# A pair of blocks 1 and 0, earlier joins, and turning inside products, in a two-layer graph kernel

## The chip, the cores and the metric

The kernel runs on one core of a Trainium2 chip. The metric is the time of one execution on the device, in microseconds (us). The engines are named as in the profile: PE is TensorE (matrix products), DVE is VectorE, ACT is ScalarE, POOL is GpSimd, and SP is SyncE, which here only issues transfers. Every engine works through its own list of instructions in a fixed order, which is settled when the kernel is built.

## The reference

The input is x (2708 x 1024, float32) and adj (2708 x 2708, only zeros and ones, with few ones and very uneven rows). Two layers follow one another, and the output is that of the second.

```python
# layer 0
q = x @ W_q.T + b_q;  k = x @ W_k.T + b_k;  v = x @ W_v.T + b_v
z = (1 / sqrt(1024)) * (q @ k.T) * adj
z = where(z == 0, -10000, z)
x = layernorm(x + relu(softmax(z, axis=1) @ v))
# layer 1
x = layernorm(x + adj @ (x @ weight) + bias)
```

A row takes part only in the products with its neighbours, the ones of its row in adj. A row without neighbours gets the mean of all v.

## The kernel before

The rows are sorted by their number of neighbours into 22 blocks of 128 rows (the last has 20), and the list SLOTS (L32) says how many neighbours a block's rows have at most. Blocks 0 to 7 are one family, blocks 8 to 21 another, each from heavy to light; block 21 has no neighbours. The 32 heaviest rows of block 0, the "hub", have their neighbours dealt over four times as many lanes, and their shares are joined later.

The kernel never forms q, k and v of all rows. For layer 0 it takes M, the product of the transposed W_q with W_k (L609), while VectorE lists the ones of adj. Then y = x M, with a bias row, block by block of x in its given order (y_block, L288: products L319, eviction by VectorE L323, write to memory; loads of x at L280). The score of a row with a neighbour is the dot product of the row of y and the row of x (VectorE, L813). The softmax weights sum the neighbours' rows of x into a row r (VectorE, L870), and only r is multiplied by W_v. Rows without neighbours take the mean of x, whose columns are summed by ScalarE from the blocks of x in y_block (column_sums, L330 and L332) and scaled by VectorE (L294, L295). Layer 1 likewise sums the neighbours' rows of x1, layer 0's output in memory (sum_rows, L1226, VectorE at L1238 and L1241), and then multiplies by the weight.

Neighbours' rows are fetched by GpSimd, which issues one indirect transfer per slot of a block (L343, L349): 128 rows, 512 KB. It also scatters finished rows (L703).

To be multiplied, r must be turned: TensorE transposes four pieces of 128 x 128 into one of three banks (pool p_tr, L716), ScalarE copies the bank out (L717), and so twice for a block. Block 0 is turned and joined with its hub at once, by products with matrices of ones and zeros that carry the shares' weights (flip_shares, L729 to L731). Accumulating products have four banks (pool p_o).

There are three kinds of product in layer 0. A single block ("v") takes 16 matmuls (project, L739) and is finished by finish0 (L900). The last block's product with the mean is project_mean (L752), in four quarters that are put together at L761. A pair ("p") of blocks takes seven products of halves instead of eight, each of 4 matmuls (half_products, L999), in the manner of Strassen: it needs four sums of quarters of the two turned blocks (S, L988 to L991, VectorE), three differences of quarters of W_v and one quarter overwritten by a difference (L1136 to L1139, VectorE, once), and seven additions (L1011, VectorE). finish_pair (L1063) adds x and takes the sums for the norm (L1069). A norm ends on ScalarE with a square (L775), small steps in turn on ScalarE and VectorE, and a scaling (L788); then GpSimd scatters the rows.

Layer 1 goes through units of two blocks (L1221; the first unit is block 20 alone): sum_rows for later units, a unit turned (turn1, L1267), the seven products (work1, L1271, sums L1278), finish1. The row of x1 that is added comes by an accumulating transfer onto a copy of the bias that ScalarE makes (gather_x1, L1247 and L1251).

Order: layer 0 is a list of steps (L1084 to L1091) in which y blocks, single blocks and pairs stand, and a list of jobs, the attention of one piece of a block each. A loop (L1119 to L1171) goes through the steps, gives each a credit of time and runs jobs while there is credit, then turns what this step and the next need, then writes the step's products. A scheduler sorts each engine's instructions by this order and their dependencies; instructions in a block `high_priority(URGENT)` are moved ahead. The joining of the hub's and block 0's shares (attend_shares, L954 to L971) advances a stage every second step. In each of layer 0's pairs and layer 1's units, turn_pair (L977) writes both the turning and the sums S of the next pair ahead of the present pair's products:

```python
            for k, c in steps[i:i + 2]:
                if k != "y" and c not in turned and not (left_y and k == "p"):
                    turned[c] = turn0(c) if k == "v" else turn_pair([lambda rT, r=got[b_]: flip(r, rT) for b_ in c], xb_pools[0])
                    done0.update(blocks_of((k, c)))
```

The code that may be run instead when the lists do not hold the graph (dense_part) is not run here.

Of the kernel before, what the change touches and what calls it, by code (L numbers as in the profile page):

```python
# [80 lines left out]
def sparse_part(ctx, tc, x, xT, adj, wqT, wkT, wvT, bq, bk, bv, w1, b1, out):  # L81
# [29 lines left out]
    with es:  # L111
# [159 lines left out]

        def load_x():
            b = len(xts)
            if b == NB:
                return
            r0, n = b * P, rows[b]
            xt = xa.tile([P, DC, P], F32, name="xt", bufs=3)
            if n < P:
                nc.gpsimd.memset(xt, 0.0)
            nc.sync.dma_start(out=xt[:, :, :n], in_=xT[:, r0:r0 + n].rearrange("(c p) n -> p c n", p=P))  # L280
            xts.append(xt)
# [6 lines left out]
        def y_block(b):  # L288
            r0, n = b * P, rows[b]
            xt = xts[b]  # L290
            if b == NB - 1:
                column_sums(b)

                nc.vector.tensor_reduce(xbT, xs, AX.X, ALU.add)  # L294
                nc.vector.tensor_scalar_mul(xbT, xbT, 1.0 / N)  # L295
# [34 lines left out]
        def column_sums(b, behind=None):  # L330
            for c in range(DC):
                put = nc.scalar.activation(junka, xts[b][:, c, :], AF.Copy, accum_out=xs[:, c, b:b + 1])  # L332
# [580 lines left out]
        def attend_shares(b, got):  # L913
# [43 lines left out]
            nc.vector.tensor_add(tops, tr[:, 0, :], far)  # L957
            nc.vector.tensor_reduce(top, tops, AX.X, ALU.min)
            turn = stat.tile([P, 1], F32, name="turn")
            nc.scalar.activation(turn, nm, AF.Exp, bias=top, scale=-1.0)  # L960
            nc.vector.tensor_tensor(den, den, turn, op=ALU.mult)
            nc.vector.tensor_scalar(tops, far, 0.0, None, op0=ALU.is_equal)
# [14 lines left out]
        def turn_pair(flips, pool):  # L977
# [5 lines left out]
            if len(flips) == 1:  # L983
                return A, None
# [7 lines left out]
            return A, S  # L992
# [20 lines left out]
        def pair_products(A, S, w, ts, base, to, whole, first_alone=False):  # L1013
# [10 lines left out]
            whole(0, 0, pb, to[0][0])  # L1024
            if first_alone:
# [27 lines left out]
        def project_pair(pair, A, S):  # L1053
# [6 lines left out]
            pair_products(A, S, wv_q, wv_t, [bias, bias], [halves_of(t) for t in ts], whole, pair == pairs[-1])  # L1060
# [24 lines left out]
        pairs = [(7, 20), (19, 18), (17, 8), (16, 11), (15, 10), (9, 14), (13, 12)]  # L1085
# [5 lines left out]
        steps += [("v", b) for b in [1, 0] + last] + [("p", pair) for pair in pairs]  # L1091
# [22 lines left out]

        credit = -STEP
# [3 lines left out]
        for i, (kind, b) in enumerate(steps):  # L1119
# [23 lines left out]
            while 0 in jobs and i >= 15:  # L1143
                credit -= run_job()
# [4 lines left out]
            for k, c in steps[i:i + 2]:  # L1149
                if k != "y" and c not in turned and not (left_y and k == "p"):  # L1150
# [493 lines left out]
```

## Time and profile before

| what | before |
|---|---|
| median of 9 runs | 1067.93 us (1066.31 to 1073.64) |
| the profiled execution | 1063.92 us |
| its span, first to last instruction | 1062.2 us |
| TensorE busy, 0 to 120 (M, lists of adj) | 113.9 of 120.0 us |
| 120 to 520.74 (rest of M, y, first blocks of layer 0) | 388.9 of 400.7 us |
| 520.74 to 746.39 (rest of layer 0) | 221.3 of 225.7 us |
| 746.39 to 758.35 (x1 becomes complete) | 0.3 of 12.0 us |
| 758.35 to 1044.25 (layer 1) | 278.6 of 285.9 us |
| 1044.25 to 1062.20 (end) | 0.7 of 18.0 us |

The profiled execution is one run, 4.0 us under the median; what lies around its span is 1.7 us.

How the lines of a profile are read. The page's first line has, for each engine, its busy time, the share of the span and the number of instructions (PEld is the loading of weights, which overlaps PE). A line of a timeline has start, duration, engine, line of the code, operation, output and inputs by their names in the code, shape and number of instructions, and in square brackets how long the engine was idle before and what ended that. A line of a table by stretches has the stretch and its length, then for PE, PEld, DVE, ACT and POOL the busy time with the number of instructions, then the mean clock that TensorE was granted (1.00 is full), the share of time in which the transfer engines were busy, and GB/s. A line of the chain (the work that ended last, followed back from the end) has start, duration and what it was; "issue" is time in which an engine waited for nothing that the profile shows.

### The profile page before, as it was taken

How to read it: one execution, taken by the hardware profiler on the slowest of the kernel's cores; microseconds unless marked ns; L12 is line 12 of the kernel's file. 1: busy time of each engine (PE TensorE's matmuls, PEld its weight loads, DVE VectorE, ACT ScalarE, POOL GpSimd, SP SyncE). 2: the span in 40 equal slices, each digit the busy share in tenths (PEclk: the TensorE clock that was granted, in tenths of full speed). 3: DMA queues.
4: the chain of work that ended last, by engine and by line, in shares of the span. 5: the costliest groups of instructions: out<-in, count | busy, mean ns of one | idle time of the engine just before them, and what ended most of it. 6: DMA issues, size and time to landing. Idle time of an engine off the chain costs nothing.

```text
span 1062.2 us, 10216 instructions
## 1 busy us (share of the span) xinstructions
PE 1003.7 (94%) x2849; PEld 473.8 (45%) x2849; DVE 849.8 (80%) x1831; ACT 425.3 (40%) x894; POOL 490.5 (46%) x397
## 2 busy tenths in 40 slices
PE   7999999999999999999999999999589999999993
PEld 6444444444443444444545444444234444454441
DVE  8799999995297879999399999974678877996432
ACT  4688787522042332224424444332322363333321
POOL 1000140057654546526157666611578777887300
PEclk9999999999999999999999999999799999999997
DMA  9555458565887656796432777726589699979701
GB/s 354 199 205 201 166 210 290 159 216 171 293 251 254 209 183 205 228 341 195 172 118 93 241 247 259 260 94 209 155 286 260 206 279 330 297 204 317 193 40 43
DMA packets 90962, 229.20 MB, mean 216 GB/s; under 512 B 18410, under 2 KB 40394, under 8 KB 88188
## 3 DMA queue, kind: packets, MB, share of 16 engines
q0 software_dynamic: 48768, 148.05, 43.5%
q1 hardware_dynamic: 42128, 80.41, 21.8%
q8 instruction: 24, 0.39, 0.1%
q14 instruction: 42, 0.34, 0.1%
HBM read 219.61 MB, written 33.68 MB: 238 GB/s over the span
## 4 chain that ended last, share of the span: by engine, by line
PE 25%; DVE 12%; issue 5%; DMA 4%; POOL 3%; ACT 2%; POOLq 0%; DVEq 0%; ACTq 0%
PE po L999 22%; DVE r L870 3%; DVE junkv L813 2%; DMA g<-x_d,tabs 2%; DVE t L1011 1%; PE tr L716 1%; DMA yg<-y_d,tabs 1%; POOL xr L343 1%; DVE r L1241 1%; POOL g L349 1%; ACT junks L775 1%; PE po L739 1%; PE tr L729 1%; DVE t L1069 0%; DMA out_dram<-xr,tabs 0%
## 5 line engine op out<-in xcount | busy, mean ns | idle before, releaser
L319 PE MATMUL po<-m_sb,xt 128*128 128x512 f32 x672 | 292.3, 594 | 3.2 <-DVE yo L323 3.2
L319 PEld LDWEIGHTS po<-m_sb,xt 128*128 128x128 f32 x672 | 126.5, 190 | 159.5 <-issue 151.2
L813 DVE SCALAR_TENSOR_TENSOR junkv<-yg,g 128x1024 uint8<-128x1024 f32 x109 | 133.0, 1220 | 32.7 <-DMA g<-in_x_dram,tabs 14.9
L349 POOL DMA_INDIRECT g<-in_x_dram,tabs x86 | 110.8, 1288 | 71.1 <-ACT r L868 19.8
L999 PE MATMUL po<-t,s_all 128*128 128x512 f32 x272 | 122.9, 594 | 3.4 <-DVE xr L1011 3.4
L1241 DVE SCALAR_TENSOR_TENSOR r<-g,valid,r 128x1024 f32<-128x1024 f32 x77 | 98.7, 1281 | 18.9 <-DMA g<-x_d,tabs 18.0
L609 PE MATMUL po<-wk_o,wq_o 128*128 128x512 f32 x256 | 110.5, 592 | 0.0
L739 PE MATMUL po<-wv,rT 128*128 128x512 f32 x224 | 97.8, 594 | 2.9 <-DVE pr L855 2.3
L775 ACT ACTIVATE junks<-t,lnm 128x1024 uint8<-128x1024 f32 (+1 forms) x41 | 47.0, 1147 | 126.2 <-DVE lnm L773 96.1
L563 POOL DMA_INDIRECT tab_d<-rec,pos_i x22 | 27.1, 1230 | 129.6 <-DVE pos_i L552 123.2
L870 DVE SCALAR_TENSOR_TENSOR r<-g,pr,r 128x1024 f32<-128x1024 f32 x64 | 81.8, 1280 | 5.8 <-ACT r L882 4.6
L999 PE MATMUL po<-w,rT 128*128 128x512 f32 x192 | 86.4, 599 | 0.0
L349 POOL DMA_INDIRECT g<-x_d,tabs x67 | 75.6, 1128 | 22.7 <-issue 14.0
L332 ACT ACTIVATE junka<-xt 128x128 f32<-128x128 f32 x176 | 53.9, 306 | 73.7 <-PE po L319 56.7
L788 ACT ACTIVATE t<-t,nmr,rstd 128x1024 f32<-128x1024 f32 (+1 forms) x41 | 50.0, 1237 | 81.1 <-DVE nmr L787 80.9
L999 PEld LDWEIGHTS po<-t,s_all 128*128 128x128 f32 x272 | 51.2, 190 | 68.7 <-issue 58.5
L224 DVE MAX8 few<-a 128x8 f32<-128x75 f32 (+3 forms) x132 | 79.2, 618 | 0.0
L609 PEld LDWEIGHTS po<-wk_o,wq_o 128*128 128x128 f32 x256 | 48.4, 190 | 59.2 <-issue 59.0
L999 PE MATMUL po<-w,s_all 128*128 128x512 f32 x160 | 72.1, 592 | 0.0
L221 DVE SCALAR_TENSOR_TENSOR a<-a,iota 128x2708 f32<-128x2708 f32 (+1 forms) x22 | 65.2, 2964 | 5.4 <-ACT junk L220 5.4
L739 PEld LDWEIGHTS po<-wv,rT 128*128 128x128 f32 x224 | 42.3, 190 | 55.8 <-issue 54.5
L717 ACT COPY rT<-tr 128x512 f32<-128x512 f32 x80 | 43.0, 585 | 54.1 <-PE tr L716 54.1
(350 smaller groups left out, 1522.5 us busy)
## 6 DMA issues: line engine op xcount, KB each, us to landing
a<-in_adj_dram SPq DMA_DIRECT2D x21, 1354.0 KB, 5.9
xt<-in_xT_dram SPq DMA_DIRECT2D x21, 512.0 KB, 5.0
y_d<-yo SPq DMA_DIRECT2D x21, 512.0 KB, 5.7
g<-in_x_dram SPq DMA_DIRECT2D x21, 512.0 KB, 7.6
wq_i<-in_wqT_dram SPq DMA_DIRECT2D x8, 512.0 KB, 9.0
wk_i<-in_wkT_dram SPq DMA_DIRECT2D x8, 512.0 KB, 10.2
wv<-in_wvT_dram SPq DMA_DIRECT2D x16, 256.0 KB, 5.3
w<-in_w_dram SPq DMA_DIRECT2D x4, 1024.0 KB, 7.7
```

The costliest lines, as they stand in the source:

```text
L221: nc.vector.scalar_tensor_tensor(a[:n], a[:n], 1.0, iota[:n], op0=ALU.is_equal, op1=ALU.mult)
L224: nc.vector.max(few[:n, i * 8:(i + 1) * 8], a[:n, cuts[i]:cuts[i + 1]])
L319: put = nc.tensor.matmul(po, xt[:, c, :], m_sb[c // 2][:, c % 2, k0:k1], start=(c == 0), stop=(c == DC - 1))
L332: put = nc.scalar.activation(junka, xts[b][:, c, :], AF.Copy, accum_out=xs[:, c, b:b + 1])
L349: nc.gpsimd.indirect_dma_start(out=dst[:n], out_offset=None, in_=src, in_offset=bass.IndirectOffsetOnAxis(ap=at, axis=0), bounds_check=N - ...
L609: nc.tensor.matmul(po, wq_o[i // 2][:, o, i % 2 * P:(i % 2 + 1) * P], wk_o[:, o, hs], start=(o == 0), stop=(o == DC - 1))
L739: put = nc.tensor.matmul(acc, rT[:, c, :], w[c // 4][h][:, c % 4, :], start=(c == 0), stop=(c == DC - 1))
L775: nc.scalar.activation(junks[:n], t[:n], AF.Square, bias=nm[:n], accum_out=vs[:n])
L813: nc.vector.scalar_tensor_tensor(junkv[:n], yg[:n, :D], scale, xg[:n], op0=ALU.mult, op1=ALU.mult, accum_out=s)
L870: nc.vector.scalar_tensor_tensor(r[:n], xg[j][:n], pr[:n, j:j + 1], r[:n], op0=ALU.mult, op1=ALU.add)
L999: put = nc.tensor.matmul(acc, a[:, k], w[:, k], start=start and k == 0, stop=stop and k == DC // 2 - 1, skip_group_check=True)
L1241: put = nc.vector.scalar_tensor_tensor(r[:n], xg[:n], ok[:n, j:j + 1], r[:n], op0=ALU.mult, op1=ALU.add)
```

## The change

It has four parts.

1. **x of the last rows.** Block 21's 20 rows of x get a tile of their own, 32 columns wide in place of 128 (xt_last). VectorE clears it and SP loads it ahead of all other blocks of x. GpSimd's clearing of a whole tile goes. The column sums of this block read 32 columns.
2. **Order on VectorE.** The mean (a reduction and a scaling) and the five steps of the joining that lie between the transposition and the one-column product are written with high priority. Block 0's three jobs may start at step 13 in place of 15.
3. **Blocks 1 and 0 as a pair.** The steps "v" of 1 and 0 go, and (1, 0) becomes the first pair, behind the product with the mean. So there are eight pairs where there were seven, and the differences of W_v are needed earlier. Block 0 is turned with its shares inside turn_pair.
4. **Turning and sums.** turn_pair only turns; the four sums are a function of their own (pair_sums). The turning of the next pair or unit is written between the second and the third of the present pair's seven products (a call `between()`), and the sums S behind the seven. The same holds in layer 1 (for block 20 alone, behind its first half product). There, the summing of rows for units 2 and 3 is written behind the first unit's products, and each later unit starts that for three units on, as before.

The diff (before has the lines of the profile):

```diff
--- before.py
+++ after.py
@@ -269,14 +269,19 @@
         junka = xa.tile([P, P], F32, name="junka", bufs=1)
...
+        xt_last = xa.tile([P, DC, HUB], F32, name="xt_last", bufs=1)
+        nc.vector.memset(xt_last, 0.0)
+        nc.sync.dma_start(out=xt_last[:, :, :rows[-1]], in_=xT[:, (NB - 1) * P:].rearrange("(c p) n -> p c n", p=P))
         def load_x():
...
             r0, n = b * P, rows[b]
+            if b == NB - 1:
+                xts.append(xt_last)
+                return
             xt = xa.tile([P, DC, P], F32, name="xt", bufs=3)
-            if n < P:
-                nc.gpsimd.memset(xt, 0.0)
             nc.sync.dma_start(out=xt[:, :, :n], in_=xT[:, r0:r0 + n].rearrange("(c p) n -> p c n", p=P))
...
@@ -291,8 +296,9 @@
             if b == NB - 1:
...
-                nc.vector.tensor_reduce(xbT, xs, AX.X, ALU.add)
-                nc.vector.tensor_scalar_mul(xbT, xbT, 1.0 / N)
+                with tc.high_priority(URGENT):
+                    nc.vector.tensor_reduce(xbT, xs, AX.X, ALU.add)
+                    nc.vector.tensor_scalar_mul(xbT, xbT, 1.0 / N)
             yo = yos[b % 2]
...
             if b == NB - 1:
@@ -329,7 +335,7 @@
...
             for c in range(DC):
-                put = nc.scalar.activation(junka, xts[b][:, c, :], AF.Copy, accum_out=xs[:, c, b:b + 1])
+                put = nc.scalar.activation(junka[:, :xts[b].shape[2]], xts[b][:, c, :], AF.Copy, accum_out=xs[:, c, b:b + 1])
                 if behind is not None and c % 2 == 0:
...
@@ -954,12 +960,13 @@
             tr = p_tr.tile([P, 4, P], F32, name="tr")
...
             tops = stat.tile([P, P], F32, name="tops", bufs=1)
-            nc.vector.tensor_add(tops, tr[:, 0, :], far)
-            nc.vector.tensor_reduce(top, tops, AX.X, ALU.min)
-            turn = stat.tile([P, 1], F32, name="turn")
-            nc.scalar.activation(turn, nm, AF.Exp, bias=top, scale=-1.0)
-            nc.vector.tensor_tensor(den, den, turn, op=ALU.mult)
-            nc.vector.tensor_scalar(tops, far, 0.0, None, op0=ALU.is_equal)
+            with tc.high_priority(URGENT):
+                nc.vector.tensor_add(tops, tr[:, 0, :], far)
+                nc.vector.tensor_reduce(top, tops, AX.X, ALU.min)
+                turn = stat.tile([P, 1], F32, name="turn")
+                nc.scalar.activation(turn, nm, AF.Exp, bias=top, scale=-1.0)
+                nc.vector.tensor_tensor(den, den, turn, op=ALU.mult)
+                nc.vector.tensor_scalar(tops, far, 0.0, None, op0=ALU.is_equal)
             yield
...
             nc.tensor.matmul(mm[:, :1], tops, den, start=True, stop=True)
@@ -980,8 +987,11 @@
             for k, flip_to in enumerate(flips):
...
                 A.append(flip_to(rT))
-            if len(flips) == 1:
-                return A, None
+            return A
+        def pair_sums(A):
+            if len(A) == 1:
+                return None
             (a11, a12), (a21, a22) = [(a[:, :DC // 2], a[:, DC // 2:]) for a in A]
...
             S = [s_all[:, i] for i in range(4)]
@@ -989,7 +999,7 @@
             nc.vector.tensor_sub(S[1], S[0], a11)
...
             halves_turned.append(nc.vector.tensor_sub(S[3], a12, S[1]))
-            return A, S
+            return S
...
             return [wm_pool.tile([P, DC // 2, HALF], F32, name=f"t{k}", tag=f"m{k - 2}") for k in (2, 3, 4)]
@@ -1010,7 +1020,8 @@
             with tc.high_priority(URGENT):
...
-        def pair_products(A, S, w, ts, base, to, whole, first_alone=False):
+        def pair_products(A, S, w, ts, base, to, whole, between, first_alone=False):
...
@@ -1022,6 +1033,7 @@
             add(to[0][0], pa, base[0][0])
...
             whole(0, 0, pb, to[0][0])
+            between()
             if first_alone:
...
                 add(to[1][1], pc, base[1][1])
@@ -1050,14 +1062,14 @@
         def halves_of_turned(a):
...
-        def project_pair(pair, A, S):
+        def project_pair(pair, A, S, between):
             ts = [(xb_pools[0] if k else wp).tile([P, D], F32, name="t", bufs=2 + k) for k in range(2)]
...
-            pair_products(A, S, wv_q, wv_t, [bias, bias], [halves_of(t) for t in ts], whole, pair == pairs[-1])
+            pair_products(A, S, wv_q, wv_t, [bias, bias], [halves_of(t) for t in ts], whole, between, pair == pairs[-1])
             return ts
...
         def finish_pair(pair, ts):
@@ -1082,13 +1094,13 @@
         running = {}
...
         jobs = [6, 5, 4, 3, 2, 2, 1, 1, "hub", "hub", 0, 0, 0]
-        pairs = [(7, 20), (19, 18), (17, 8), (16, 11), (15, 10), (9, 14), (13, 12)]
+        pairs = [(1, 0), (7, 20), (19, 18), (17, 8), (16, 11), (15, 10), (9, 14), (13, 12)]
         late_jobs = [7, 20, 8, 19, 18, 8, 17, 8, 16, 11, 15, 10, 20, 9, 14, 19, 13, 12, 18]
...
                  ("y", 16), ("v", 2), ("y", 17), ("y", 18), ("y", 19), ("y", 20), ("y", 21)]
-        steps += [("v", b) for b in [1, 0] + last] + [("p", pair) for pair in pairs]
+        steps += [("v", b) for b in last] + [("p", pair) for pair in pairs]
...
             return [] if step[0] == "y" else [step[1]] if step[0] == "v" else list(step[1])
@@ -1112,6 +1124,11 @@
                 return rT
...
+        def turned_pair(pair):
+            done0.update(pair)
+            return turn_pair([lambda rT, b_=b_, r=got[b_]: flip(r, rT) if b_ else flip_shares([got["hub"], r], rT) for b_ in pair], xb_pools[0])
+        sums0 = {}
         credit = -STEP
...
         pending = None
@@ -1140,16 +1157,19 @@
             for c in [c for st in steps[i:i + 3] for c in blocks_of(st) if not (left_y and c in late)]:
...
                     credit -= run_job()
-            while 0 in jobs and i >= 15:
+            while 0 in jobs and i >= 13:
                 credit -= run_job()
...
             for k, c in steps[i:i + 2]:
-                if k != "y" and c not in turned and not (left_y and k == "p"):
-                    turned[c] = turn0(c) if k == "v" else turn_pair([lambda rT, r=got[b_]: flip(r, rT) for b_ in c], xb_pools[0])
-                    done0.update(blocks_of((k, c)))
+                if k == "v" and c not in turned and not (left_y and c in last):
+                    turned[c] = turn0(c)
+                    done0.add(c)
+            if kind == "v" and steps[i + 1][0] == "p":
+                turned[pairs[0]] = turned_pair(pairs[0])
+                sums0[pairs[0]] = pair_sums(turned[pairs[0]])
             if kind == "y":
...
                     row_constants(1)
@@ -1168,7 +1188,11 @@
             else:
...
                     pair_x[b_] = gather_x(x, b_)
-                pending = finish_pair, b, project_pair(b, *turned[b])
+                following = steps[i + 1][1] if i + 1 < len(steps) else None
+                pending = finish_pair, b, project_pair(b, turned[b], sums0[b], lambda: turned.update(
+                    {following: turned_pair(following)} if following else {}))
+                if following:
+                    sums0[following] = pair_sums(turned[following])
         w1_q = quarters_of("w1")
...
             for j in range(2):
@@ -1268,7 +1292,7 @@
             return turn_pair([lambda rT, b=b, r=r: flip_shares([(part, to_h), (r, to_0)], rT) if b == 0 else flip(r, rT)
...
-        def work1(unit, A, S, xrs):
+        def work1(unit, A, S, xrs, between):
...
             sums = [[stat.tile([P, 1], F32, name=f"sm{h}", bufs=6) for h in range(NH)] for _ in unit]
@@ -1288,19 +1312,21 @@
                 pa, pb = bank(), bank()
...
                 add(x0[1], pa, x0[1])
+                between()
                 half_products(pb, a11, t1, stop=False)
...
             else:
-                pair_products(A, S, w1_q, w1_t, xs_, xs_, whole, unit == units[-1])
+                pair_products(A, S, w1_q, w1_t, xs_, xs_, whole, between, unit == units[-1])
             return ts, sums
...
         turned1[0] = turn1(units[0], got1.pop(0))
+        sums1 = {0: pair_sums(turned1[0])}
         follow(nc.vector.tensor_sub(t1, t1, w11), firsts[0], same=True)
...
         nc.vector.tensor_sub(t3, t2, w11)
@@ -1310,15 +1336,18 @@
             for p in pending:
...
             if i + 1 < len(units):
-                turned1[i + 1] = turn1(units[i + 1], got1.pop(i + 1))
                 xrs[i + 1] = [gather_x1(b, k) for k, b in enumerate(units[i + 1])]
-            if i == 0:
-                got1[2] = [sum_rows(b, k, halves_turned[-1]) for k, b in enumerate(units[2])]
-            if i + 3 < len(units):
+            if 0 < i < len(units) - 3:
                 got1[i + 3] = [sum_rows(b, k) for k, b in enumerate(units[i + 3])]
...
                 sum_rows("hub")
-            pending = list(zip(unit, *work1(unit, *turned1.pop(i), xrs.pop(i))))
+            pending = list(zip(unit, *work1(unit, turned1.pop(i), sums1.pop(i), xrs.pop(i), lambda: turned1.update(
+                {i + 1: turn1(units[i + 1], got1.pop(i + 1))} if i + 1 < len(units) else {}))))
+            if i + 1 < len(units):
+                sums1[i + 1] = pair_sums(turned1[i + 1])
+            if i == 0:
+                for u in (2, 3):
+                    got1[u] = [sum_rows(b, k, halves_turned[-1]) for k, b in enumerate(units[u])]
             if i == 2:
...
                     pending.append((b, gather_x1(b), None))
```

## The prediction

> **What bounds the kernel now.** I read the totals of each engine first, then the chain of work that ended last, then the busy time by stretch, then the timelines of TensorE (PE), VectorE (DVE) and ScalarE (ACT) where the change works.
>
> ```profile
> PE 1003.7 (94%) x2849; PEld 473.8 (45%) x2849; DVE 849.8 (80%) x1831; ACT 425.3 (40%) x894; POOL 490.5 (46%) x397
> ```
> ```profile
> 701.91 44.65 PE po L999 x104
> ...
> 778.79 7.44 DMA g<-x_d,tabs
> 786.33 1.30 DVE r L1241
> ```
> ```profile
> 528.70:700.80 172.10, 168.37 (x526) 78.83 (x525) 168.32 (x342) 65.75 (x123) 105.31 (x73) 1.00 0.58 194
> ```
>
> TensorE is busy for 94% of the span and the chain goes through it after 701.91, so its time counts one for one there. Behind y, however, the third line gives 168.4 us of TensorE and 168.3 us of VectorE in 172.1 us: both are full. In layer 1 the chain starts with a gather and VectorE's sum of it.
>
> ```profile
> 522.44 1.98 PE L739 MATMUL po<-wv,rT 128*128 128x512 f32 x4 [0.54 <-ACT rT L717]
> ...
> 577.66 3.60 PE L999 MATMUL po<-t,s_all 128*128 128x512 f32 x8
> 581.10 3.60 PE L999 MATMUL po<-wv,s_all 128*128 128x512 f32 x8
> ...
> 671.53 1.06 PE L716 MATMUL tr<-ident,r 128*128 128x128 f32 x8 [1.37 <-DVE r L870]
> ...
> 700.85 1.06 PE L716 MATMUL tr<-ident,r 128*128 128x128 f32 x8 [1.27 <-DVE r L870]
> ...
> 758.35 1.94 PE L716 MATMUL tr<-ident,r 128*128 128x128 f32 x8 [11.69 <-DVE r L1238]
> ...
> 791.10 3.70 PE L999 MATMUL po<-t,s_all 128*128 128x512 f32 x8 [2.92 <-DVE xr L1011]
> ...
> 866.33 0.66 PE L716 MATMUL tr<-ident,r 128*128 128x128 f32 x4 [1.53 <-ACT rT L717]
> ```
>
> A half product (4 matmuls) starts 3.44 after the one before it (577.66 to 581.10). A bracket is idle time and what ended it: behind y TensorE waits for VectorE's rows r, in layer 1 once for ScalarE's copy of a turned block.
>
> I count from E = 520.74, where the last product of y ends on TensorE; layer 0 ends at 746.39, E+225.65. The idle rows between are 0.54, 0.20, 0.16, 1.37, 0.21, 0.47 and 1.27, in all 4.22.
>
> **Up to E.** The block of 20 rows waits 0.65 at 511.02 for its transfer of x. This is loaded at the start now, so the wait goes: -0.65. The small transfer is now ahead of the first 512 KB of x and of adj on SP's queue; those land in 5.0 and 5.9 us, 80 KB are a sixth of the first, so at most 0.8 of delay, and TensorE has 110.5 us of L609 before it needs x: I take 0 (0 to 0.8). GpSimd loses a memset of 0.96, VectorE gains one, both aside. Joining raised in VectorE's order puts a ScalarE exponent behind column sums, and TensorE's one-column product L965 waits for it; between 0 and one pair of sums (0.43 each): 0.3. Up to E: -0.35.
>
> **Behind E, TensorE's work.** Blocks 1 and 0 were 32 matmuls, 8 half products; as a pair they are 7: -3.44.
>
> **A new wait.** The order of the changed kernel puts the turning of the mean and its product (3.66 at 548.57) first behind y; the flips of block 1 come after. Until the mean is there TensorE has nothing else.
>
> ```profile
> 523.64 0.34 DVE L294 TENSOR_REDUCE xbT<-xs 128x8 f32<-128x176 f32 x1 [0.97 <-ACT junka L332]
> ...
> 528.79 1.29 DVE L870 SCALAR_TENSOR_TENSOR r<-g,pr,r 128x1024 f32<-128x1024 f32 x1 [4.61 <-ACT r L882]
> ```
>
> Before, ScalarE's last ten column sums start at E-2.3, after a product of y, with 0.43 from one to the next. Now eight of them read 32 columns; the read of the sum stays, so I take 0.41 each (0.3 to 0.43). 2 x 0.43 + 8 x 0.41 end at E+1.85, and reduce and scale with their gap (0.55) at E+2.45. So 2.45 of wait (1.6 to 2.9). All rows of r can come as they like, TensorE alone would end layer 0 at 225.65 - 4.22 - 3.44 + 2.45 = E+220.4: -5.2.
>
> **VectorE, the second bound.** A pair needs four sums S (L988 to L991, 0.60 each: 2.4), seven adds where two blocks had four (3 x 0.60 = 1.8) and four L1069 (0.68 with the read) for two L908 (1.15): +0.4. The order brings some 0.8 more of adds ahead of the last row: 5.4 in all. Given back: the differences of wv can start at E+4.9, when the product of the mean has read the quarter that the first one overwrites, in the 4.61 of idle time that ended at 528.79 (E+8.05): 3.1. In the stretch above it is idle for 3.8, of which I take 1.4 to remain: 2.4. The last row (block 12), before at E+180.0, is then ready at 180.0 + 5.4 - 3.1 - 2.4 = E+179.9. A score (L813) that waits for a gather of y now stands before rows of blocks 7 and 20. The gather was served by 532.38 (E+11.6), and t2 is done at E+9.3: up to 2.3 more. Behind the last flip stand 11.5 half products now (13 in the chain's 701.91 row, x104 records of 8): 0.1 + 0.9 + 39.5 gives the end of layer 0 at E+220.4 to E+222.7, -5.2 to -2.9. Where TensorE gets there at the same time I take the middle: **-4.0**.
>
> Later x1 of blocks 1 and 0 costs nothing: it is first gathered some 150 us later. The sums S are hidden under two half products (6.9 us) now instead of in front of them.
>
> **Layer 1.** The start is set by the gathers (landing at 786.33) as before; without L988 to L991 in front, I take -0.2. Then two effects with opposite signs. The wait of 1.53 at 866.33 goes, as flips are placed two half products into the unit before. But the copies that empty a group of transposes now stand on ScalarE where finishing of the last unit also stands:
>
> ```profile
> 860.18 1.15 ACT L775 ACTIVATE junks<-t,lnm 128x1024 uint8<-128x1024 f32 x1 [0.89 <-DVE lnm L773]
> ...
> 863.35 1.05 ACT L1251 COPY xr<-bias 128x1024 f32<-128x1024 f32 x1 [1.92 <-DMA out_dram<-xr,tabs]
> ...
> 865.72 0.56 ACT L717 COPY rT<-tr 128x512 f32<-128x512 f32 x1
> ```
>
> This is the wait of 866.33 from ScalarE's side: the copy at 865.72 comes after a square and a bias copy that waited. In the changed order, for unit (17,16), a square (L775) of block 19 stands before all four copies of (15,1). It waits for a mean on VectorE, and there behind two sums (1.28) of gathered rows of block 2. Three groups of transposes have a bank (p_tr), the fourth waits for the first copy. Below: 0.45 if the rows have landed; above: 1.94 (wait at 782.65 for such a gather) + 1.28 = 3.2, with some slip 3.5. The rows in between (waits of 0.42 to 1.94, plus 1.28) have 2.5 as their middle; I take 2.5, and 0.4 for the unit after. Net: -0.2 - 1.53 + 2.5 + 0.4 = **+1.2** (-1.7 to +2.2). The turn between the layers (746 to 758) and the tail are as they were.
>
> **Sum.** -0.35 - 4.0 + 1.2 = -3.15: 1063.92 becomes 1060.8 in the profiled execution. That one lies 4.0 below the median of 1067.93, so the median goes to **1064.8** (ends -4.9 to -1.2).
>
> The new waits matter twice if TensorE slows down after them. Here 11.69 of idle time were followed by 1.94 for eight transposes (1.04 elsewhere), while 2.92 were followed by 3.70 for 3.60: a tenth. The Trainium skill ("TensorE: Matmul & The Clock Gate", what's actually happening) says that the clock halves after an idle window of about 3.4 us and comes back after as much work. This speaks against putting ScalarE's queue in front of the flips; by it a wait at the upper end would cost an estimated 1.7 more, and one of 2.5 nothing, if the window didn't catch it. The trace agrees as far as its two rows reach; the sum above holds none of it.
>
> **Rivals.**
> (1) *Nothing waits.* VectorE keeps ahead and the squares are early: -0.35 - 5.2 - 1.7 = -7.3, 1060.6. For: VectorE's idle times fit its extra work. Against: both engines are full in the same stretch.
> (2) *VectorE becomes the bound of layer 0.* Its 5.4 aren't given back: last row at E+185.4, end at E+225.9, +0.25; with E and layer 1: +1.1, 1069.0. For: 168.3 of 172.1, and the rows at 671.53 and 700.85 already wait for it.
> (3) *Slower: ScalarE's queue order.* The square before the copies recurs; the order shows it at (19,18), (17,16), (15,1) and later units. At three units of 3.2 each layer 1 is 9.6 - 1.7 = +7.9, and the whole +3.5: 1071.4. It decides from the third such wait on (two: +0.3). Against: from 900 to 1000 TensorE is busy for 99.94 of 100, and gathers there run ahead.
> (4) *It does not do what it says*: flips inside products run where they ran. Then 1067.9; the order speaks against it.
>
> **How the numbers follow.** Forecast 0.42, rival 1 0.28, rival 2 0.15, rival 3 0.13, rival 4 0.02. A difference under 0.3% (3.2 us) can hardly be told from none here. The forecast lies on that bound, so I split it, 0.20 faster and 0.22 same. Faster: 0.20 + 0.28 = 0.48; same: 0.22 + 0.15 + 0.02 = 0.39; slower: 0.13. Range: from just under rival 1 (1060.0) to 1071.0, past rival 2 and short of rival 3.
>
> **What would show it.** Right: no idle row in front of the block of 20 rows; a wait of about 2.5 on xbT at the end of y; seven half products per pair from E+13 on; idle rows on r near 670 to 700 of 2.3 or less in sum; in the unit (17,16) an idle row of 2 to 3 in front of a transpose, released by a ScalarE copy; none of 1.53 later. Wrong: waits on r that grow by more than 4 (rival 2), ScalarE releases at three units (rival 3), or no such row at all (rival 1).

## The result, and the profile after

| what | before | after |
|---|---|---|
| median | 1067.93 us (31 runs) | 1079.34 us (10 runs, 1073.65 to 1081.39) |
| ratio, 95% interval | | 1.0094 (1.0076 to 1.0113) |
| profiled execution | 1063.92 us | 1079.41 us |
| end of the last product of y | 520.91 | 528.82 |
| from there to layer 1's first transposition | 237.44 us | 233.40 us |
| from there to the last product of layer 1 | 286.62 us | 298.26 us |

The change makes the kernel slower by 10 to 11 us (0.94% by the ratio, 11.4 between the medians). In the profiled executions it is 15.5, of which y ends 7.9 later, the rest of layer 0 gives 4.0 back, and layer 1 takes 11.6 more. The profiled execution of before is 4.0 under its median and that of after is at its median, so the distance of medians is the smaller one.

The first line of the page, the totals of each engine, reads much as before:

```profile
PE 1007.4 (93%) x2841; PEld 474.6 (44%) x2841; DVE 854.6 (79%) x1843; ACT 423.5 (39%) x894; POOL 495.0 (46%) x396
```

TensorE has 8 matmul records fewer (the half product) and is busy 3.7 us longer. So it must have run slower somewhere. The timeline of TensorE in the stretches named above shows where (idle time in brackets):

```profile
476.54 0.27 PE L961 MATMUL tr<-ident,nm 128*128 128x128 f32 x1
480.36 0.44 PE L961 MATMUL tr<-ident,nm 128*128 128x128 f32 x1 [3.54 <-DVE nm L940]
480.59 28.96 PE L325 MATMUL po<-m_sb,xt 128*128 128x512 f32 x64
...
513.36 0.38 PE L972 MATMUL mm<-den,tops 128*128 128x1 f32 x2 [1.01 <-DVE den L968]
...
530.72 0.62 PE L190 MATMUL tr<-ident,xbT 128*128 128x128 f32 x4 [1.91 <-DVE xbT L301]
...
709.88 1.06 PE L722 MATMUL tr<-ident,r 128*128 128x128 f32 x8 [1.27 <-DVE lnm L779]
```

Two transpositions of the joining stand one behind the other, and the second waits 3.54 for VectorE. That is block 0's, which in the kernel before stands behind 64 more records of y:

```profile
474.63 0.27 PE L955 MATMUL tr<-ident,nm 128*128 128x128 f32 x1
474.74 27.63 PE L319 MATMUL po<-m_sb,xt 128*128 128x512 f32 x64
...
502.35 0.30 PE L955 MATMUL tr<-ident,nm 128*128 128x128 f32 x1
```

The 64 records of y take 28.96 after the wait (27.63 before). The three figures, 3.54 + 1.33 + 1.01, are 5.9 of the 7.9 by which y ends later; another wait, 0.94 at 420.63, is new too, and the rest is spread. The wait for the mean is there (1.91), and the last wait on a row is 1.27, as before.

```profile
791.65 0.66 PE L722 MATMUL tr<-ident,r 128*128 128x128 f32 x4 [2.45 <-ACT rT L723]
794.12 5.26 PE L1009 MATMUL po<-t,s_all 128*128 128x512 f32 x8 [1.81 <-DVE xr L1021]
...
804.75 3.70 PE L1009 MATMUL po<-t,s_all 128*128 128x512 f32 x8 [1.94 <-DVE xr L1021]
...
822.02 1.47 PE L722 MATMUL tr<-ident,r 128*128 128x128 f32 x12
827.12 0.66 PE L722 MATMUL tr<-ident,r 128*128 128x128 f32 x4 [3.63 <-ACT rT L723]
827.61 5.30 PE L1009 MATMUL po<-t,s_all 128*128 128x512 f32 x8
...
856.85 0.66 PE L722 MATMUL tr<-ident,r 128*128 128x128 f32 x4 [1.17 <-ACT rT L723]
...
912.57 0.66 PE L722 MATMUL tr<-ident,r 128*128 128x128 f32 x4 [2.60 <-ACT rT L723]
```

In layer 1, at four units three groups of transposes are done (x12) and the fourth waits for ScalarE's copy of the first: 2.45, 3.63, 1.17 and 2.60. At three of them a half product takes 5.3 where it takes 3.6 elsewhere (for the first, a wait of 1.81 on an addition comes in between). All idle rows of layer 1 after its first transposition sum to 13.6 (7.15 before), and TensorE is busy 284.6 in it (279.4): 6.4 of waiting and 5.2 of slower work make the 11.6.

What the copy waits for is read from ScalarE's and VectorE's timelines of the wait of 3.63:

```profile
824.79 1.15 ACT L781 ACTIVATE junks<-t,lnm 128x1024 uint8<-128x1024 f32 x1 [3.87 <-DVE lnm L779]
...
826.50 2.03 ACT L723 COPY rT<-tr 128x512 f32<-128x512 f32 x4
```
```profile
816.15 1.28 DVE L1265 SCALAR_TENSOR_TENSOR r<-g,valid,r 128x1024 f32<-128x1024 f32 x1 [3.53 <-DMA g<-x_d,tabs]
...
823.36 1.27 DVE L1265 SCALAR_TENSOR_TENSOR r<-g,valid,r 128x1024 f32<-128x1024 f32 x1
824.55 0.20 DVE L779 TENSOR_SCALAR lnm<-sm,sm 128x1 f32<-128x1 f32 x1
```

The four copies stand behind a square, the square waits 3.87 for its mean (lnm), and the mean stands on VectorE behind sums of gathered rows, one of which waited 3.53 for its gather. This is the chain that the prediction described for the unit (17,16), and it was read at this unit alone.

And the clock that TensorE was granted in 5 or 6 us after such a wait, from the table by stretches (the clock is the third number from the end):

```profile
480.00:485.00 5.00, 4.64 (x9) 2.17 (x10) 5.00 (x11) 2.48 (x12) 1.44 (x1) 0.67 0.77 277
485.00:490.00 5.00, 5.00 (x13) 2.21 (x12) 5.00 (x9) 3.23 (x14) 0.32 (x1) 1.00 0.90 294
...
827.00:833.00 6.00, 5.88 (x13) 2.80 (x14) 4.86 (x10) 3.17 (x8) 3.76 (x3) 0.72 0.98 189
833.00:838.00 5.00, 5.00 (x13) 2.19 (x12) 2.73 (x8) 2.37 (x2) 2.29 (x2) 1.00 0.56 216
```

It is 0.67 and 0.72 of full speed, and full again in the next stretch.

### The profile page after: what moved, and what is told of

It reads as the page before. It is cut to its first block, busy times and chain, and to the rows that moved or that the text cites. A ratio compares the mean times of both kernels' runs of the same rounds, so it can differ in the third digit from the quotient of the medians.

```text
span 1077.6 us, 10205 instructions
## 1 busy us (share of the span) xinstructions
PE 1007.4 (93%) x2841; PEld 474.6 (44%) x2841; DVE 854.6 (79%) x1843; ACT 423.5 (39%) x894; POOL 495.0 (46%) x396
## 4 chain that ended last, share of the span: by engine, by line
DVE 37%; PE 24%; issue 16%; DMA 10%; POOL 9%; ACT 3%; POOLq 0%; SPq 0%; DVEq 0%; ACTq 0%
PE po L1009 19%; DVE a L221 6%; DVE few L224 5%; DVE junkv L819 5%; DVE r L876 4%; POOL g L355 3%; DMA g<-in_x_dram,tabs 3%; DMA g<-x_d,tabs 3%; DVE t L1021 2%; POOL xr L349 1%; DVE yo L329 1%; POOL tab_d L569 1%; DVE t L1081 1%; PE tr L722 1%; PE tr L246 1%
## 5 line engine op out<-in xcount | busy, mean ns | idle before, releaser
L1009 PE MATMUL po<-t,s_all 128*128 128x512 f32 x288 | 135.7, 612 | 3.8 <-DVE xr L1021 3.7
L355 POOL DMA_INDIRECT g<-x_d,tabs x67 | 82.0, 1224 | 22.7 <-issue 17.1
L1009 PEld LDWEIGHTS po<-t,s_all 128*128 128x128 f32 x288 | 54.4, 196 | 66.4 <-issue 59.1
L338 ACT ACTIVATE junka<-xt 128x128 f32<-128x128 f32 x168 | 51.4, 306 | 71.1 <-PE po L325 56.8
L745 PE MATMUL po<-wv,rT 128*128 128x512 f32 x160 | 69.7, 593 | 3.2 <-DVE pr L861 2.3
L1009 PE MATMUL po<-t,rT 128*128 128x512 f32 x144 | 64.7, 592 | 0.0
L722 PE MATMUL tr<-ident,r 128*128 128x128 f32 x320 | 42.1, 278 | 24.1 <-DVE r L1262 11.7
## 6 DMA issues: line engine op xcount, KB each, us to landing
wk_i<-in_wkT_dram SPq DMA_DIRECT2D x8, 512.0 KB, 11.7
```

The costliest lines, as they stand in the source:

```text
L338: put = nc.scalar.activation(junka[:, :xts[b].shape[2]], xts[b][:, c, :], AF.Copy, accum_out=xs[:, c, b:b + 1])
L355: nc.gpsimd.indirect_dma_start(out=dst[:n], out_offset=None, in_=src, in_offset=bass.IndirectOffsetOnAxis(ap=at, axis=0), bounds_check=N - ...
L722: nc.tensor.transpose(tr[:, k, :], r[:, c * P:(c + 1) * P], ident)
L745: put = nc.tensor.matmul(acc, rT[:, c, :], w[c // 4][h][:, c % 4, :], start=(c == 0), stop=(c == DC - 1))
L1009: put = nc.tensor.matmul(acc, a[:, k], w[:, k], start=start and k == 0, stop=stop and k == DC // 2 - 1, skip_group_check=True)
```

## The experiments

The changed kernel is the base of nearly all. From the fifth experiment on they have block 0's jobs from step 15, as the first and the third, and are read beside these; only the eighth starts from the kernel before, and one repeats the changed kernel. The kernels were measured in series, each beside the kernel before on one chip. Before is at 1067.93 in the series of the result and at 1068.07 in the last four experiments, but at 1078.38 to 1080.26 in the three series between. The profiles show where those ten us lie: from 255 to 280 us TensorE is busy for 25.0 us in all six profiles of the two shorter series, and for 15.7 to 18.6 in all twelve of the three longer ones, at a granted clock of 0.73 to 0.85 and with nothing visible that it waits for ("issue"). It gets through 27 to 35 records there in place of 59 or 60, which at 0.43 each makes 11 to 14 us. All that lies ahead of the rows read here, and its cause is open. So ratios to before are compared. Lengths of a stage come from one execution each and scatter: with the same order, layer 1 lasted 288.4 to 294.9.

**Block 0's jobs from step 15.**

```diff
-            while 0 in jobs and i >= 13:
+            while 0 in jobs and i >= 15:
```

> The changed kernel, with block 0's jobs again from step 15 on instead of 13. Theory A: because the third piece of block 0 starts two steps earlier, its transposition moves from in front of the last y blocks (502.35 before) to right behind the hub's, where TensorE waits 3.54 for VectorE's row constant, is then 1.33 slower over the next 64 records, and waits another 1.01 at the one-column product; y ends 8.0 later than before. Without it those 5.9 us go: about 1073.5, and the idle row in front of the second transposition is gone. Rival B: the delay comes from the joining's high priority or from the early load of the last rows' x, and moves only elsewhere: 1078 to 1080.

Measured 1.0025 (1.0008 to 1.0042), 1081.03 us against 1078.61. The idle row at the second transposition and that at the one-column product are gone. They are in all four profiles with the jobs from step 13 (3.5 to 4.9 together) and in none of those from 15. The size is best taken from the second and third experiment, of one series, which differ by this line alone: 1080.01 - 1073.62 = 6.4, or 0.6%; across series it is 0.4 to 0.7%. So theory A is right on the mechanism and near on the size (5.9). The absolute time missed because of the ten us above. Repeated at 1068.07, it is 1.0032, and there y ends at 521.68 (528.82 in the changed kernel, 520.91 before).

**Layer 1 as before.** The next unit's flips and sums S go back ahead of the unit's products, and the summing of rows for units 2 and 3 goes back to where it was; so the flips' place is not tried by itself:

```diff
             if i + 1 < len(units):
+                turned1[i + 1] = turn1(units[i + 1], got1.pop(i + 1))
+                sums1[i + 1] = pair_sums(turned1[i + 1])
                 xrs[i + 1] = [gather_x1(b, k) for k, b in enumerate(units[i + 1])]
...
-            pending = list(zip(unit, *work1(..., lambda: turned1.update(...))))
+            pending = list(zip(unit, *work1(..., lambda: None)))
```

> The changed kernel, with layer 1 written as before (flips and sums of the next unit ahead of the present unit's products). Theory A: layer 1's 11.6 us more are made there, by flips that wait inside the products; they go, about 1068 (11 less than the changed kernel), and layer 1 lasts 286 to 287 from its first transposition to the last product. Rival B: they come from layer 0's later or denser end (rows of x1 that arrive later, gathers that queue), then layer 1 stays above 294 and the time above 1075.

Measured 1.0018 (0.9992 to 1.0043). Layer 1 lasts 289.4 from its first transposition to its last product: theory A by its time (rival B had 294 or more), somewhat over the 286 to 287 that the profiled execution of before, which lies 4.0 under its median, suggested. The same order of layer 1 took 294.5 and 294.9 in the third and seventh experiment and 288.4 in the last, against 296.7 to 298.3 with the flips inside in four profiles; the medians are the firmer measure.

**Both undone.**

> Both of the former: jobs from step 15, layer 1 as before. What is left of the change is the early x of the last rows, the joining's and the mean's place on VectorE, the pair (1, 0), and flips inside products in layer 0. Theory A: layer 0 behind y is 4.1 shorter than before, y ends 0 to 2 later: 1063.8 to 1066, faster than the kernel before by 2 to 4. Rival B: the gain behind y existed only because y ended late and VectorE had caught up meanwhile; then waits on r come back near the end of layer 0 and the time is 1067 to 1070.

Measured 0.9957 (0.9934 to 0.9979): faster than the kernel before, by 0.4% there; in the repetition below 0.9975. Beside the first experiment's kernel, of the same series, layer 1's form is worth 7.4 us. The three ratios fit: 1.0025 + 1.0018 - 0.9957 = 1.0086, against 1.0094 and, once more measured, 1.0074.

**Copies first.** In layer 1 finishing is written behind the flips, and a square may stand only behind the last copy of a turned block:

```diff
             put = nc.scalar.activation(junks[:n], t[:n], AF.Square, bias=nm[:n], accum_out=vs[:n])
+            if in_layer1:
+                follow(put, copies[-1], same=True)
```

> The changed kernel, with layer 1's norm of the last unit behind the flips on ScalarE: finishing is written after the flips, and each square must stand behind the last copy of a turned block. Theory A (ScalarE's order): the four waits on copies (2.45, 3.63, 1.17, 2.60) and most of the slower products after them (1.66, 1.70, about 1.9) go; two waits on VectorE's additions near the start (1.81, 1.94) may stay or grow by up to 3: 1068 to 1071. Rival C: the copies stand late because the rows r or VectorE are late there; the same waits come back with VectorE's rows as releaser: 1076 or more.

Measured 1.0191 (1.0153 to 1.0229): slower than the changed kernel. The profile of this kernel (an execution 6.3 under the median of five), TensorE in layer 1:

```profile
801.29 0.66 PE L724 MATMUL tr<-ident,r 128*128 128x128 f32 x4 [1.92 <-ACT rT L725]
803.99 5.20 PE L1013 MATMUL po<-t,s_all 128*128 128x512 f32 x8 [2.04 <-DVE xr L1025]
...
848.65 3.70 PE L1013 MATMUL po<-t,rT 128*128 128x512 f32 x8 [2.45 <-DVE t L1306]
...
968.68 0.74 PE L737 MATMUL tr<-to,r 128*128 128x96 f32 x2 [7.66 <-DVE r L1269]
```

The waits on copies are gone but for the first, and others came: 2.45 on VectorE's last additions, and 7.66 on block 0's row. GpSimd, which in the changed kernel has four waits of 0.9 to 3.9 in this stretch, has none above 0.31 here, and still block 0's row, with its 15 gathers and 11 for the hub, is late. Theory A falls in the form "put the copies first", and rival C is right that others are as late. That the late norms hold up what follows them is likely, but not shown.

**A fourth bank in layer 1.** TensorE's and ScalarE's order stay as they are; the fourth group goes to a bank that was free by then:

```diff
-                tr = p_tr.tile([P, 4, P], F32, name="tr")
+                turns[0] += 1
+                last_group = turns[0] >= 0 and turns[0] % 4 == 3
+                tr = p_mm.tile([P, 4, P], F32, name="mm") if last_group else p_tr.tile([P, 4, P], F32, name="tr")
```

> The changed kernel with jobs from step 15 (as the first experiment, which stood at 1.0025 of the kernel before on its chip) and in layer 1 a fourth bank for the fourth group of transposes; the order on TensorE and ScalarE is the same. Theory A: what TensorE waited for inside the products was a free bank, and nothing it needed: the waits on ScalarE copies (1.85, 3.63, 0.89, 2.60 in the first experiment) and the slower products after them (about 5 in all) go, 6 to 13 us: 0.990 to 0.997. Rival C: the rows and sums of VectorE are as late, and TensorE waits for them a few products later: 1.000 or more.

Measured 0.9992 (0.9957 to 1.0026), between the two theories, and by its interval not told from the first experiment. Not one wait on a copy is left, but the idle rows of layer 1 sum to 11.7 (12.1 in the first experiment):

```profile
797.63 6.72 PE L1015 MATMUL po<-t,s_all 128*128 128x512 f32 x8 [4.39 <-DVE xr L1027]
...
835.97 3.70 PE L1015 MATMUL po<-t,s_all 128*128 128x512 f32 x8 [1.83 <-DVE xr L1027]
...
863.37 3.70 PE L1015 MATMUL po<-t,s_all 128*128 128x512 f32 x8 [1.35 <-DVE xr L1027]
```

The third product accumulates onto the first's bank and so waits for the addition that reads it; on VectorE this addition stands behind sums of gathered rows, as the mean did:

```profile
794.37 2.61 DVE L1271 SCALAR_TENSOR_TENSOR r<-g,valid,r 128x1024 f32<-128x1024 f32 x2 [0.77 <-DMA g<-x_d,tabs]
796.89 0.68 DVE L1027 TENSOR_TENSOR xr<-po,xr 128x512 f32<-128x512 f32 x1
```

So with the bank free, the wait shows one step further on.

**The same bank with layer 1 as before.**

> The third experiment's kernel (jobs from step 15, layer 1 as before; 0.9957) with the same fourth bank in layer 1. Theory A: its two waits on copies (2.30 and 2.11) go, and nothing else: 0.991 to 0.994. Rival C: no change, 0.995 to 0.997.

Measured 0.9971 (0.9942 to 1.0001): no gain over 0.9957. The two waits on copies are gone, and waits on VectorE came (2.68 and 1.98). This is nearest to rival C.

**The pair alone.** Jobs and layer 1 as before, and in layer 0 also the flips and sums ahead of the products:

```diff
+                if following:
+                    turned[following] = turned_pair(following)
+                    sums0[following] = pair_sums(turned[following])
                 for b_ in b:
                     pair_x[b_] = gather_x(x, b_)
```

> The third experiment's kernel with the flips and sums of the next pair written ahead of the present pair's products in layer 0, as before; what is left of the change is the pair (1, 0), the early x and the order on VectorE. If the gain behind y (4.1) is the half product alone (3.4, less the new wait for the mean), this is at 0.996 to 0.997, like the third. If placing the flips inside the products saves the waits on r (4.2 before, 1.9 in the third), it is 2 to 3 us worse: 0.998 to 0.999.

Measured 0.9963 (0.9927 to 1.0000), the same as 0.9957, and from the end of y to layer 1 it takes 232.9 as the third experiment does. So what layer 0 gains is there without the flips' new place, which adds nothing that shows.

**The early x and the order on VectorE alone.**

> The kernel before with the early x of the last rows and the high priority of the mean and the joining alone. Theory: the wait of 0.65 goes and nothing else moves, -0.3 to -0.9 us: 0.999 to 1.000. Rival: the load at the head of the queue delays the first x, or the priority pushes other work on VectorE: over 1.001.

Measured 1.0002 (0.9971 to 1.0033). The wait at the block of 20 rows is gone; the time can't be told from before.

**Half of layer 1's rows.** In both forms the second half of the slots of layer 1's sums is left out:

```diff
-            for j in range(tab.shape[1] if b else J0):
+            for j in range(((tab.shape[1] if b else J0) + 1) // 2):
```

> The first experiment's kernel (jobs from step 15, flips inside the products of layer 1) with half of the neighbours' rows left out of layer 1's sums, so half of its gathers and of VectorE's sums. To be read beside the next one, which is the same with layer 1's flips as before; with all rows the two stood 0.7% (7.3 us) apart, the flips inside being slower. Theory G: what stands in ScalarE's and TensorE's way are instructions of VectorE that stand behind sums that wait for gathers; with half the gathers these waits go, and the two are within 2 us. Rival A: the order on ScalarE alone makes the waits; the distance stays at 5 us or more.

> The third experiment's kernel (jobs from step 15, layer 1's flips ahead of the products as before) with half of the neighbours' rows left out of layer 1's sums. Theory G: it is within 2 us of the former. Rival A: 5 us or more faster than the former. Both leave a part of layer 1 out, so only their distance is read.

Measured 1.0027 (1.0004 to 1.0051) and 1.0010 (0.9985 to 1.0035): 1.9 us apart. The distance is the one that theory G gave, but for another reason: neither kernel became faster than with all rows, and layer 1's idle rows sum to 16.5 and 15.1. The first has waits of 6.51 and 3.63 on copies. With half the gathers, the instructions are ordered anew, and means and additions still stand behind single sums, one of which waits 7.94 for its gather. So fewer gathered rows alone do not take the waits away; as the order changed with them, the experiment doesn't separate the two forms.

**Flips in front of the last product in layer 1.** `between()` is called ahead of the seventh product instead of behind the second.

> The first experiment's kernel (1.0025 on its chip), where in layer 1 the next unit's flips stand in front of the last of the seven products instead of behind the second, 14 us later. If layer 1 loses because rows, means and copies are wanted before the gathers have brought what VectorE has in front of them, most of the 7 us come back: 0.996 to 0.999, and the waits on copies at the early units are 1 us or less. If it loses because the sums S and the copies come inside the products at all, it stays at 1.001 to 1.004.

Measured 1.0010 (0.9986 to 1.0034), at the lower end of the second range, with an interval that reaches into the first: inconclusive. Layer 1 lasts 296.8 (297.3 in the first experiment). The first unit's wait on a copy became one of 6.63 on an addition, another of 2.83 stands at a later addition, and only one on a copy is left (1.08).

**The changed kernel again.**

> The changed kernel once more, beside the others on their chip, since chips differ by some ten us. It was 1.0094 of the kernel before; the first three experiments were 1.0025, 1.0018 and 0.9957, so the two undone parts cost 0.7% each and add up to 0.013 + 0.9957 = 1.009. Expected 1.006 to 1.011; below 1.004 the parts would not add up.

Measured 1.0074 (1.0053 to 1.0095). Its waits on copies in layer 1 are 2.14, 3.41, 0.78, 0.67 and 2.59, much as in the first profile.

**Means first, then means and bank, beside the first and third kernel.** In layer 1 the norm's small steps on VectorE get high priority:

```diff
+            with ahead():
                 nc.vector.tensor_scalar(nm[:n], sm[:n], sm2[:n], -1.0 / D, op0=ALU.add, op1=ALU.mult)
...
+            with ahead():
                 nc.vector.scalar_tensor_tensor(ve[:n], vs[:n], D * EPS, near[:n], op0=ALU.add, op1=ALU.mult)
```

> The first experiment's kernel with the small steps of layer 1's norms (mean, its negation times the inverse deviation, and what lies between) at high priority on VectorE: in its order the means of unit (19,18) stand in front of the sums of block 2 instead of behind two of them. Theory V: the squares that TensorE waits for through ScalarE's copies are late because their means stand behind sums that wait for gathers; then the waits on copies shrink to under 1.5 each and the time falls by 4 to 7 us beside the first experiment's kernel of the same call. Rival P: the means cannot be earlier, since the products and additions they come from are late themselves; 0 to 2 us.

> The former with the fourth bank of transposes in layer 1 too. With the bank alone the waits moved to VectorE's additions (4.39, 1.83, 1.35). Theory V: those additions too stand behind sums, which this does not move: 0 to 3 us faster than the former. Rival P: no difference to the former, and both at the first experiment's time.

> The first experiment's kernel once more, as the measure of the two former on the same chip: 1.0025 of the kernel before on another chip; expected 1.001 to 1.004.

> The third experiment's kernel once more: 0.9957 of the kernel before on another chip; expected 0.994 to 0.998, and 6 to 8 us under the first experiment's kernel of the same call. If the distance is under 3 us, layer 1's part of the loss is not what the first two experiments seemed to show.

| kernel (before: 1068.07) | median | ratio, interval | layer 1, first transposition to last product |
|---|---|---|---|
| means first | 1070.63 | 1.0024 (1.0001 to 1.0047) | 294.4 |
| means and bank | 1068.23 | 0.9998 (0.9982 to 1.0014) | 292.8 |
| jobs from 15 | 1072.86 | 1.0032 (1.0018 to 1.0046) | 297.0 |
| both undone | 1066.32 | 0.9975 (0.9958 to 0.9992) | 288.4 |

Layer 1's part is 6.5 us in this series. Means alone bring 2.2, which the intervals don't tell from nothing (and which is nearer to rival P than to theory V); means and bank bring 4.6, with intervals that don't meet. So two thirds of layer 1's loss go with the bank and the means' place together (4.3 of 8.6, half, by the stage lengths of one execution each); what makes the last 1.9 is open, and the intervals don't tell it from nothing. The waits on copies with the means first are 2.64 and 0.59, where the kernel with the jobs from 15 has 2.09, 5.65, 0.56, 0.84 and 2.00. But its idle rows still sum to 12.0 (11.9 in that kernel), since others, 5.02 on an addition above all, took their place; with means and bank they sum to 9.1. The last kernel is the fastest of this table, 1.8 us under before.

## Why the prediction was wrong

**Up to E, forecast -0.35, measured +7.9: a part of the change was not priced.** The diff lets block 0's jobs start at step 13. The working costed the transfer, the memsets and the priorities, and of the joining only its one-column product; the earlier jobs have no term, and so a cost of nothing without a reason. The order of TensorE's instructions had the answer: both L955 transpositions, 64 records of y apart before, stand next to one another after (L961 there). The second waits for a number that VectorE makes after block 0's third piece, and 3.54 of waiting, 1.33 of slower products and 1.01 at the one-column product follow. Undoing that one line shows it: the rows vanish, and the time falls by 0.6%. For that product the working had 0.3, for an exponent behind column sums on ScalarE; the releaser was that, and the size three times as large. The wait that the early x was to remove (0.65) is gone; that the time fell with it is not shown (1.0002 by itself).

**Behind E, forecast -4.0, measured -4.04.** That the two agree to 0.04 is luck: with the pair, this stretch lasts 232.3 to 235.8 in sixteen profiles, 1.6 to 5.2 less than in the one of before. Within that the sum held, with terms that were a little off: the wait for the mean is 1.91 (2.45 forecast, bounds 1.6 to 2.9), the waits on rows sum to 2.5, and TensorE's work is 4.2 shorter (3.44 forecast). The reason given for the middle value, flips later by two half products, is not shown: without it the stretch is as long.

**Layer 1, forecast +1.2 with an upper end of +2.2, measured +11.6.** The mechanism was the one described, square in front of the copies and its mean behind sums of gathered rows, and at the unit named it cost 3.63 (2.5 taken, 3.5 the end). What failed is the count: one unit and a remainder of 0.4 for the next in the forecast, four units and 9.85 in the trace. That was the rival on the slower side ("at three units of 3.2 each"). What was held against it, that TensorE is busy for 99.94 of 100 us between 900 and 1000, was read in the kernel before, where flips stand ahead of the unit's products; the change moves the time at which copies are needed, so that row says nothing on it (97.40 in the changed kernel). The slower products after the waits (5.2) were left out of the sum, though 758.35 showed that they exist.

The range ended at 1071.0 because each rival was priced by itself. Here the forecast layer 0 and the rival's layer 1 came together with a cost that nobody had listed. The ends given with the sum, -4.9 to -1.2, are also narrower than those of its terms, which add up to about -7.3 and -1; how they were reached is not said.

The sentence on the Trainium skill ("TensorE: Matmul & The Clock Gate", what's actually happening) put the limit at an idle window of about 3.4 us. The runs here agree with a loss of 1.3 to 1.9 per wait in the changed kernel (3.1 once, in the kernel with the further bank), near the 1.7 estimated, but not with that length as a limit. After the wait of 2.60 at 912 the clock was 0.72 for 6 us, and two shorter ones in the kernel with means and bank were followed by half products of 5.40:

```profile
788.03 3.70 PE L1022 MATMUL po<-t,s_all 128*128 128x512 f32 x8 [2.57 <-DVE xr L1034]
...
797.11 5.40 PE L1022 MATMUL po<-t,s_all 128*128 128x512 f32 x8 [1.94 <-DVE xr L1034]
...
834.02 5.40 PE L1022 MATMUL po<-t,rT 128*128 128x512 f32 x8 [2.30 <-DVE t L1315]
```

The wait of 2.57 in the same kernel and that of 2.92 in the kernel before were followed by 3.70. The measurement decides: a wait of 2 to 3 us may cost nearly as much again, or nothing.

What stays open: the last third of layer 1's loss, and why the changed layer 1 does no better when its flips stand later. Not tried: the new place of the summing for units 2 and 3 by itself, and the sums of gathered rows on another engine.

## What to carry to other kernels

Price every line of a diff, also the one that only changes when something may begin, and look in the order of the instructions at what then stands in front of the bound engine: there, an instruction moved earlier waits for its input, and all behind it wait too. When turning is moved inside the products, its copies come due earlier as well; look at what stands ahead of them on every engine in the chain (copy, square, mean, sum, gather), at each unit and not at one. A change of several parts can hold its gain in one: the pair (with the early x and the order on VectorE, which by themselves showed nothing) is worth 0.25 to 0.4%, and the other parts cost some three to five times that.

## What the runs showed of the hardware

A wait of TensorE can be paid twice. After 3.54 idle the next 5 us ran at a granted clock of 0.67, after 3.63 the next 6 us at 0.72, and the half product behind the latter took 5.3 instead of 3.6. How long a wait must be isn't fixed: 1.94 and 2.30 sufficed once, 2.57 and 2.92 once did not.

The same program was some 10 us slower in three of five series (the kernel before: 1067.9 and 1068.1, but 1078.4, 1078.6 and 1080.3), as much as the whole effect that was asked for, so only ratios within a series tell it. In the profiles it lies in one stretch, 255 to 280 us, where TensorE stood idle for 6.4 to 9.3 us without a visible cause and ran at 0.73 to 0.85 of its clock. Whether it goes with the chip is open: no chip on record was used in two series.
